# A patch gather on TensorE: from f32 one-hots made on ScalarE to three bf16 parts with one-hots shared between VectorE and ScalarE

## The chip, the core and the metric

The kernel runs on one core of one Trainium2 chip. The metric is the device time of one execution in microseconds (us); less is better. The kernel before took 6811.16 us, the median of three runs (6809.01 to 6819.06).

## What is computed

The input is `x`, 8 images of 32 channels and 128 x 128 pixels. Two layers follow each other. The reference, cut to the part that the change touches and to the outline of the rest:

```python
def _patch_match_stack(x):                 # x is group-normalised
    for dy in range(-2, 3):                # 25 offsets
        for dx in range(-2, 3):
            d = ((x - sh) ** 2).sum(1, keepdims=True)   # sh: x shifted by (dy, dx), clipped
            costs.append(_conv(d, ones, pad=1))         # 3x3 box sum
    _, idx = jax.lax.top_k(-cost, K)       # K = 8 cheapest offsets of each pixel
    g = x[:, yy, xx]                       # gather: 8 pixels of 32 channels for each pixel
    return g as [8, 256, 128, 128]
xb = _patch_match_stack(_gn(x))
dct = _conv(xb, dct_w, groups=32)
h = relu(dw3x3(_conv(xb, w1), w2)); h = relu(dw3x3(_conv(h, w3), w4))
wiener = sigmoid(dw3x3(_conv(h, w5), w6))              # 256-channel 1x1 and depthwise 3x3
x = x + _conv(_conv(wiener * dct, inv_dct_w, groups=32), agg_w)   # layer 0
x = x + conv5x5(_gn(x))                                           # layer 1
```

## The kernel before, in words

**Order of the work.** The order of the instructions on TensorE, VectorE and ScalarE is written out by the program, and each of these engines works its list from front to back. `steps` holds 17 steps for each image: 16 blocks of 8 rows and a last short one. One pass of the outer loop treats four depths of the pipeline, `i` in (3, 2, 1, 0): the three pairs of a pointwise and a depthwise convolution of successive steps, and the end of layer 0. In every `i` the loop also places one `unit` of the gather and calls `tick`, which takes work of the next image (its search for offsets) and of layer 1 from four queues: D (VectorE), A (ScalarE), P and Q (TensorE). Work on D carries a planned cost, and `total` (line 992) sets how much of it a tick releases. In `turn`, used before the main loop and wherever `until` waits for a condition, each queue is run once.

**Search.** For each image `prep` normalises the pixels (`xn`, f32, four strips of 32 rows on the partitions) and pushes `sources`. `squares` makes 36 pairs of differences (L421 on VectorE, squares on ScalarE, sums over channels on TensorE); `costs` makes four blocks of box sums, each with 32 calls of max and max_index (L513, L514). `places` turns the indices into numbers of rows of a gather table and sends them to DRAM as bf16 (`idxd`, L549).

**Gather table.** `sources` transposes the pixels in f32, eight chunks of four rows with four transposes each (L390), copies them from PSUM (`xs`, L392), writes them to DRAM pixel by pixel (`xl`, L394), and from there makes `xtd` with 16 + 2 DMAs (L402, L406). `xtd` holds, for every row, 16 column positions (`QW`) of 11 column tiles (`NT`), each tile 12 columns wide (`TW`). These DMAs are issued on GpSimd's queue, like most of the kernel's. The step that follows in the queue is taken once for each chunk.

**Gather.** A unit is four rows and half (`g`) of the eight offsets. `gather_load` brings the table of the rows (`xt`, 8 rows x 16 positions on 128 partitions, L567) and two broadcasts of the indices to all partitions (`ib`, 128 x 1024 bf16 each, L582). `gather_select` makes the one-hot on ScalarE in two passes, max(0, 1 - (index - partition)^2): a square with the partition number as bias (L596), and a Relu that writes f32 (`sel`, L597). `gather_pixels` multiplies: 11 column tiles x 4 strips of 32 output partitions, each an f32 matmul of a 128 x 32 table with 48 one-hot columns (L611; 32 columns in the last tile), and copies the result to `xb` (L618). An f32 matmul stands in the trace as two records, so a unit has 88. The main loop selects unit u+1, loads unit u+3 and multiplies unit u. There are 64 units for each image, 512 in all.

**What reads it.** `xb` feeds the first pointwise convolution (L649, L673) and, by way of DRAM, the grouped 1x1 convolution at the end (L769, L788). The depthwise convolutions are split: half of the channels on TensorE (L729), half as eight multiply-adds on VectorE (L703).

Of the kernel before, what the change touches and what calls it, by code (L numbers as in the profile page):

```python
# [15 lines left out]
P = 128  # L16
# [4 lines left out]
NS = H // R  # L21
TW = 12
NT = 11
QW = TW + 4
HR = 38
HX = W + 4
SR = 6
EPS = 1e-5


# [12 lines left out]
def bm3d_conv_preact(  # L43
# [88 lines left out]
    nc.vector.memset(neg, 0.0)  # L132
    nc.vector.tensor_copy(neg[:, 28:32], cst[:, C_B + 24 : C_B + 24 + P : 32])
    nplace = const.tile([P, 1], F32, name="nplace")
    nc.vector.tensor_scalar(nplace, cst[:, C_Q : C_Q + 1], -1.0, None, op0=ALU.mult)

# [245 lines left out]
    def sources(b, xn):  # L382


        xl = dram.tile([H, W, C], F32, name=f"xl_{b}", tag="xl")
        for r in range(0, 32, 4):
            yield "P", 0
            pt = ps_x.tile([P, 4, P], F32, name=f"px_{b}_{r}", tag="x")
            for q in range(4):
                nc.tensor.transpose(pt[:, q], xn[:, 3 + r + q, 2 : 2 + W], ident)  # L390
            xs = work.tile([P, 4, P], F32, name=f"xs_{b}_{r}", tag="ct")
            nc.scalar.copy(xs, pt)  # L392
            for q in range(4):
                nc.gpsimd.dma_start(  # L394
                    xl.rearrange("(g r) x c -> r x g c", g=4)[r + q],
                    xs[:, q].rearrange("p (g c) -> p g c", c=C),
                )
        xt = xtd[b] = dram.tile([H, QW, NT, C], F32, name=f"xtd_{b}", tag="xtd")
        for j in range(QW):
            ta, tz = (1 if j < 2 else 0), (NT if j < 10 else NT - 1)  # L400
            xa = TW * ta + j - 2
            nc.gpsimd.dma_start(  # L402
                xt[:, j, ta:tz], xl[:, xa : xa + TW * (tz - ta - 1) + 1 : TW]
            )
        for ja, jz, t, at in ((0, 2, 0, 0), (10, QW, NT - 1, W - 1)):
            nc.gpsimd.dma_start(  # L406
                xt[:, ja:jz, t], xl[:, at : at + 1].to_broadcast([H, jz - ja, C])
            )

# [109 lines left out]
    def places(b, idx, i):  # L519


        if i == 0:
            idxd[b] = dram.tile([4, 8, K * 4, W], BF16, name=f"idxd_{b}", tag="idxd")
        yield "D", 2.6
# [8 lines left out]
        for lim in (10.0, 15.0, 20.0):  # L533
# [5 lines left out]
            o3,  # L539
            cst[:, C_BASE : C_BASE + 4].unsqueeze(1).to_broadcast([P, 64, 4]),  # L540
            ALU.add,
        )
        yield "P", 0
        for h in range(2):
            pt = ps_x.tile([P, 512], F32, name=f"pi_{b}_{i}_{h}", tag="x")
            nc.tensor.transpose(pt[:, :P], o[:, h * P : (h + 1) * P], ident)
            li = work.tile([P, P], BF16, name=f"li_{b}_{i}_{h}", tag="li")
            nc.scalar.copy(li, pt[:, :P])
            nc.gpsimd.dma_start(  # L549
                idxd[b][2 * h : 2 * h + 2, 2 * i : 2 * i + 2].rearrange("g s k x -> g (s k) x"),  # L550
                li,
            )
        ready.add((b, i))
        if i == 3:
            ready.add(b)

    ready = set()
    xbs, xts, ibs, selss = {}, {}, {}, {}

    def gather_load(b, s4, g):  # L560

        if g == 0:

            xt = xts[b, s4] = work.tile([P, NT, C], F32, name=f"xt_{b}_{s4}", tag="xt", bufs=3)
            ys = [min(max(4 * s4 - 2 + r, 0), H - 1) for r in range(8)]
            if ys[7] - ys[0] == 7:
                nc.gpsimd.dma_start(  # L567
                    xt.rearrange("p t c -> p (t c)"),
                    xtd[b][ys[0] : ys[0] + 8].rearrange("r x t c -> (r x) (t c)"),
                )  # L570
            else:
                for r, y in enumerate(ys):
                    nc.gpsimd.dma_start(
                        xt[QW * r : QW * (r + 1)].rearrange("p t c -> p (t c)"),
                        xtd[b][y].rearrange("x t c -> x (t c)"),
                    )
        for k2 in range(2):
            ib = work.tile(
                [P, 2, 4, W], BF16, name=f"ib_{b}_{s4}_{g}_{k2}", tag="ib", bufs=5
            )  # L580
            k0 = 4 * g + 2 * k2
            nc.gpsimd.dma_start(  # L582
                ib.rearrange("p k y x -> p (k y x)"),
                idxd[b][s4 // 8, s4 % 8, 4 * k0 : 4 * k0 + 8]
                .rearrange("k x -> (k x)")
                .partition_broadcast(P),
            )
            ibs[b, s4, g, k2] = ib

    def gather_select(b, s4, g, k2=(0, 1)):  # L590
        for k2 in k2:
            sel = work.tile(
                [P, 2, 4, W], F32, name=f"sel_{b}_{s4}_{g}_{k2}", tag="sel", bufs=4
            )
            ib = ibs.pop((b, s4, g, k2))
            nc.scalar.activation(ib, ib, AF.Square, bias=nplace)  # L596
            nc.scalar.activation(sel, ib, AF.Relu, scale=-1.0, bias=1.0)  # L597
            selss[b, s4, g, k2] = sel

    def gather_pixels(b, s4, g):  # L600

        n, h = s4 // 2, s4 % 2
        if h == 0 and g == 0:
            xbs[b, n] = xbp.tile([P, 2, R, W], F32, name=f"xb_{b}_{n}", tag="xb")
        xb, xt = xbs[b, n], xts[b, s4]
        sels = [selss.pop((b, s4, g, k2)) for k2 in range(2)]
        pg = ps_x.tile([P, 4, W], F32, name=f"pg_{b}_{s4}_{g}", tag="x")
        for t in range(NT):
            xa, xz = TW * t, min(TW * (t + 1), W)
            for j in range(4):  # L610
                nc.tensor.matmul(  # L611
                    pg[C * j : C * (j + 1), :, xa:xz],
                    xt[:, t],
                    sels[j // 2][:, j % 2, :, xa:xz],
                    start=True,
                    stop=True,
                )
        nc.scalar.copy(xb[:, g, 4 * h : 4 * h + 4], pg)  # L618
        if h == 1 and g == 1:
            nc.gpsimd.dma_start(xbd[b][:, :, R * n : R * (n + 1)], xb)  # L620
# [305 lines left out]
    def middle(b, mr):  # L926
# [40 lines left out]
    units = [  # L967
        (b, 2 * n + h, g) if n < NS else None
        for b, n in steps
        for h in range(2)  # L970
        for g in range(2)
    ]
# [3 lines left out]
    def unit(stage, u, *rest):  # L976
        if 0 <= u < len(units) and units[u]:
            if stage is gather_load:
                at = (units[u][0], units[u][1] % 8 // 2)
                until(lambda: at in ready, 4.0)  # L980
            stage(*units[u], *rest)
# [9 lines left out]

    total = 5.5 + 3.3 + 36 * 1.95 + 4 * 4.6 + 32 * 1.85 + 4 * 2.6 + 4 * 3.6 + 6.6
    owed = [0.0]
# [19 lines left out]
    with tc.manual_schedule(engines=ORDERED):  # L1013
# [19 lines left out]
        for s in range(len(steps) + 2):  # L1033
# [10 lines left out]
            for i in (3, 2, 1, 0):  # L1044
# [22 lines left out]
                if s < len(steps):  # L1067
                    unit(gather_select, u + 1, (0,))
                    unit(gather_load, u + 3)
# [11 lines left out]
                if s < len(steps):  # L1081
                    unit(gather_select, u + 1, (1,))
                    u += 1
# [72 lines left out]
```

## Time and profile before

| | |
|---|---|
| median of the runs | 6811.16 us |
| the profiled execution: span from its first to its last instruction | 6807.3 us |
| what lies between that span and the median | 3.9 us |
| TensorE matmul busy | 6354.3 us, 93% |
| VectorE busy | 5860.4 us, 86% |
| ScalarE busy | 5064.6 us, 74% |
| GpSimd busy (it issues most of the DMAs) | 3246.7 us, 48% |
| mean granted TensorE clock | 0.973 |
| DMA | 1021.41 MB, 150 GB/s |

The profile gives one execution. A busy share is the time in which an engine had an instruction in flight; a row of the profile gives a line of the kernel, the engine, the operation, output<-input, how often, then busy time and the mean duration of one. A matmul's mean duration is its flight, not the distance between two. After the bar stands the idle time of the engine in front of these instructions and what ended it. The chain is followed back from the last instruction to whatever released each one; its shares tell where a saved microsecond would have counted in this execution. The windows give the busy time of each engine in a stretch of 50 us.

### The profile page before, as it was taken

How to read it: one execution, taken by the hardware profiler on the slowest of the kernel's cores; microseconds unless marked ns; L12 is line 12 of the kernel's file. 1: busy time of each engine (PE TensorE's matmuls, PEld its weight loads, DVE VectorE, ACT ScalarE, POOL GpSimd, SP SyncE). 2: the span in 40 equal slices, each digit the busy share in tenths (PEclk: the TensorE clock that was granted, in tenths of full speed). 3: DMA queues.
4: the chain of work that ended last, by engine and by line, in shares of the span. 5: the costliest groups of instructions: out<-in, count | busy, mean ns of one | idle time of the engine just before them, and what ended most of it. 6: DMA issues, size and time to landing. Idle time of an engine off the chain costs nothing.

```text
span 6807.3 us, 257036 instructions
## 1 busy us (share of the span) xinstructions
PE 6354.3 (93%) x113378; PEld 3352.8 (49%) x113378; DVE 5860.4 (86%) x8822; ACT 5064.6 (74%) x6698; POOL 3246.7 (48%) x5351
## 2 busy tenths in 40 slices
PE   5798899999999999999999999999999999999997
PEld 1454454554545455454554455545555454455553
DVE  7789988989889898898988888899888899877776
ACT  5787778777687777877777777877769777687772
POOL 7354446444464444544445444454436554344334
PEclk8899999999999999999999999999999999999998
DMA  4566656666566675666756656566665666566653
GB/s 90 143 153 153 151 149 154 159 152 158 147 156 155 144 169 135 163 151 152 167 135 158 161 146 169 138 165 159 149 150 151 162 156 152 138 170 157 154 151 80
DMA packets 809627, 1021.41 MB, mean 150 GB/s; under 512 B 255456, under 2 KB 619936, under 8 KB 808512
## 3 DMA queue, kind: packets, MB, share of 16 engines
q0 software_dynamic: 422432, 745.61, 42.9%
q1 hardware_dynamic: 383568, 258.11, 17.4%
q8 instruction: 892, 14.61, 0.9%
q10 hardware_dynamic: 2512, 1.25, 0.1%
q14 instruction: 223, 1.83, 0.1%
HBM read 553.25 MB, written 217.01 MB: 113 GB/s over the span
## 4 chain that ended last, share of the span: by engine, by line
PE 55%; DVE 23%; ACT 8%; DMA 6%; issue 5%; POOL 3%; SPq 0%; ACTq 0%; DVEq 0%; POOLq 0%
PE pw L729 18%; DVE acc L703 15%; PE pv L649 13%; PE p L673 12%; PE pg L611 4%; DVE df L421 3%; PE pc L788 2%; DMA t<-t 2%; PE p L902 2%; ACT df L429 2%; ACT ib L596 2%; DVE idx L514 1%; PE pa L809 1%; DMA xf<-xbd 1%; DVE acc L796 1%
## 5 line engine op out<-in xcount | busy, mean ns | idle before, releaser
L703 DVE SCALAR_TENSOR_TENSOR acc<-tv,dwv,acc 128x1024 f32<-128x1024 f32 (+3 forms) x3264 | 4032.9, 1237 | 249.6 <-ACT acc L700 140.3
L729 PE MATMUL pw<-t,dwd 96*32 96x254 f32 (+7 forms) x31680 | 2144.1, 422 | 84.7 <-issue 40.5
L729 PEld LDWEIGHTS pw<-t,dwd 96*32 96x32 f32 (+1 forms) x31680 | 1103.9, 111 | 906.6 <-issue 440.7
L582 POOL DMA_DIRECT2D ib<-idxd x1024 | 570.7, 558 | 1796.5 <-ACT sel L597 1620.6
L596 ACT ACTIVATE ib<-ib,nplace 128x1024 bf16<-128x1024 bf16 x1024 | 1170.1, 1143 | 9.5 <-DMA ib<-idxd 9.5
L597 ACT ACTIVATE sel<-ib 128x1024 f32<-128x1024 bf16 x1024 | 1084.8, 1059 | 32.5
L673 PE MATMUL p<-acc,lw 128*32 128x256 f32 x16768 | 989.1, 381 | 25.3 <-ACT tv L657 22.7
L649 PE MATMUL pv<-acc,lw 128*128 128x512 f32 (+1 forms) x2112 | 980.7, 607 | 29.9 <-DVE acc L796 27.4
L769 POOL DMA_DIRECT2D xf<-xbd x1088 | 650.2, 630 | 304.2 <-PE pc L788 87.0
L673 PEld LDWEIGHTS p<-acc,lw 128*32 128x32 f32 x16768 | 556.2, 111 | 454.9 <-ACT tv L657 62.5
L657 ACT COPY tv<-pv 128x512 f32<-128x512 f32 (+2 forms) x784 | 438.1, 578 | 390.4 <-PE pv L649 374.2
L611 PEld LDWEIGHTS pg<-sel,xt 128*32 128x32 f32 x45056 | 575.5, 111 | 252.1 <-issue 54.2
L429 ACT ACTIVATE df<-df 128x786 f32<-128x786 f32 (+2 forms) x576 | 468.0, 859 | 291.9 <-DVE df L421 289.2
L611 PE MATMUL pg<-sel,xt 128*32 128x48 f32 x45056 | 592.7, 207 | 80.4 <-ACT sel L597 46.0
L421 DVE TENSOR_TENSOR df<-xn 128x786 f32<-128x786 f32 (+2 forms) x576 | 532.5, 976 | 116.0 <-PE pd L436 109.2
L742 ACT ACTIVATE acc<-pw 128x512 f32<-128x512 f32 (+2 forms) x808 | 439.9, 573 | 249.7 <-PE pw L729 249.0
L649 PEld LDWEIGHTS pv<-acc,lw 128*128 128x128 f32 x2112 | 384.2, 193 | 475.6 <-issue 398.1
L707 ACT ACTIVATE acc<-acc 128x1024 f32<-128x1024 f32 (+3 forms) x408 | 416.8, 1022 | 229.7 <-DVE acc L703 229.5
L680 ACT COPY t<-p 128x512 f32<-128x512 f32 x800 | 424.6, 570 | 127.7 <-PE p L673 125.7
L700 ACT ACTIVATE acc<-tv,dwv 128x1024 f32<-128x1024 f32 (+3 forms) x408 | 454.5, 1114 | 52.6 <-PE pa L809 35.0
L649 PE MATMUL pv<-xb,lw 128*128 128x512 f32 x1024 | 477.4, 609 | 0.0
L673 PE MATMUL p<-xb,lw 128*32 128x256 f32 x8192 | 468.1, 380 | 4.4 <-DVE xy L914 4.4
(151 smaller groups left out, 5782.5 us busy)
## 6 DMA issues: line engine op xcount, KB each, us to landing
ib<-idxd POOLq DMA_DIRECT2D x1024, 256.0 KB, 4.4
xbd<-xb POOLq DMA_DIRECT2D x128, 1024.0 KB, 6.7
xf<-xbd POOLq DMA_DIRECT2D x960, 128.0 KB, 7.3
t<-t SPq DMA_DIRECT2D x792, 128.0 KB
t<-t SPq DMA_DIRECT2D x384, 256.0 KB
tv<-tv SPq DMA_DIRECT2D x384, 130.0 KB
xt<-xtd POOLq DMA_DIRECT2D x240, 176.0 KB, 4.6
xl<-xs POOLq DMA_DIRECT2D x256, 64.0 KB, 2.6
```

The lines of the kernel that those rows point to most:

```text
L421: nc.vector.tensor_sub(df[:, :, ca:cz], xn[:, r0 : r0 + SR, ca:cz], xn[:, r0 + dy : r0 + dy + SR, ca + dx : cz + dx],)
L429: nc.scalar.activation(df[:, :, ca:cz], df[:, :, ca:cz], AF.Square)
L582: nc.gpsimd.dma_start(ib.rearrange("p k y x -> p (k y x)"), idxd[b][s4 // 8, s4 % 8, 4 * k0 : 4 * k0 + 8] .rearrange("k x -> (k x)") .part ...
L596: nc.scalar.activation(ib, ib, AF.Square, bias=nplace)
L597: nc.scalar.activation(sel, ib, AF.Relu, scale=-1.0, bias=1.0)
L611: nc.tensor.matmul(pg[C * j : C * (j + 1), :, xa:xz], xt[:, t], sels[j // 2][:, j % 2, :, xa:xz], start=True, stop=True,)
L649: nc.tensor.matmul(ps[:, :hr], lhsT[:, g, P:CK], src(g)[:, h : h + hr], start=g == 0, stop=g == 1,)
L673: nc.tensor.matmul(ps[C * r : C * (r + 1), e, :nb], lhsT[:, g, s], rows[:, r : r + 4 * nb - 3 : 4], start=g == 0, stop=g == 1,)
L700: nc.scalar.activation(acc, rows, AF.Copy, scale=tap)
L703: nc.vector.scalar_tensor_tensor(acc, rows, tap, acc, op0=ALU.mult, op1=ALU.add)
L729: nc.tensor.matmul(pt[u][C * j : C * (j + 1), ka:kz, :nb, xa:xz], dwd[0:hi, i - 1, u, j, dx + 1], t[0:hi, j, ka:kz, :nb, xa + dx : xz + dx ...
L769: nc.gpsimd.dma_start(xf[p : p + C, m, j0:j1], src[g, m, (h + m + 1) % 2, :, :, ya:yz])
```

## The change

The table is kept as three bf16 parts of each f32 number: the number rounded to bf16, the rest rounded to bf16, and the rest of that. Eight bits of mantissa each, they add up to the f32 number, and a one-hot picks each exactly; the three matmuls of a pixel add up in PSUM. `sources` makes the parts with two casts on ScalarE and two subtractions on VectorE for each chunk, transposes twelve times in bf16, copies twice from PSUM and writes 96 instead of 32 numbers for each pixel. It now goes through six steps of the queues for each chunk (A, D, A, D, P, P) where it went through one. `xtd` has 15 positions of 12 tiles, each 11 columns wide, six for the left half of the columns and six for the right (`HW` = 64); a table fills 120 partitions. It is made with 30 + 2 DMAs.

A unit is now four rows and one half of the columns (`f`), all eight offsets. It has one broadcast `ib` of 128 x 2048 bf16, held in four buffers. The one-hot of the left half is one comparison on VectorE, in place; that of the right half two passes on ScalarE, in place, bf16. A unit's matmuls are 6 tiles x 3 parts x 4 strips = 72, of 88 columns (72 in the last tile). `gather_load` waits, while the program is written out, until `sources` of its image has been placed. The indices are written in twice as many DMAs.

```diff
-TW = 12
-NT = 11
+TW = 11
+NT = 12
+HW = W // 2
+NP = 3
...
     def sources(b, xn):
-        xl = dram.tile([H, W, C], F32, name=f"xl_{b}", tag="xl")
+        xl = dram.tile([H, W, NP * C], BF16, name=f"xl_{b}", tag="xl")
         for r in range(0, 32, 4):
-            yield "P", 0
-            pt = ps_x.tile([P, 4, P], F32, name=f"px_{b}_{r}", tag="x")
-            for q in range(4):
-                nc.tensor.transpose(pt[:, q], xn[:, 3 + r + q, 2 : 2 + W], ident)
-            xs = work.tile([P, 4, P], F32, name=f"xs_{b}_{r}", tag="ct")
-            nc.scalar.copy(xs, pt)
...
+            nc.scalar.copy(parts[0], rows)
+            yield "D", 0.7
+            nc.vector.tensor_sub(rest, rows, parts[0])
+            yield "A", 0
+            nc.scalar.copy(parts[1], rest)
+            yield "D", 0.7
+            nc.vector.tensor_sub(parts[2], rest, parts[1])
+            for q0 in (0, 2):
+                yield "P", 0
+                pt = ps_x.tile([P, 2, 4, NP, C], BF16, name=f"px_{b}_{r}_{q0}", tag="x")
+                for q in range(2):
+                    for s in range(NP):
+                        nc.tensor.transpose(pt[:, q, :, s], parts[s][:, q0 + q], ident_b)
+                xs = work.tile([P, 2, 4, NP * C], BF16, name=f"xs_{b}_{r}_{q0}", tag="xs")
+                nc.scalar.copy(xs, pt.rearrange("p q g s c -> p q g (s c)"))
...
+        sourced.add(b)
...
+        ib = work.tile([P, K, 4, HW], BF16, name=f"ib_{b}_{s4}_{f}", tag="sel", bufs=4)
+        nc.gpsimd.dma_start(
+            ib.rearrange("p k y x -> p (k y x)"),
+            idxd[b][s4 % 8 // 2, s4 // 8 * 2 + s4 % 2, f].rearrange("k x -> (k x)").partition_broadcast(P),
+        )
...
-            nc.scalar.activation(ib, ib, AF.Square, bias=nplace)
-            nc.scalar.activation(sel, ib, AF.Relu, scale=-1.0, bias=1.0)
...
+        if f == 0:
+            if part != 1:
+                nc.vector.tensor_scalar(ib, ib, place, None, op0=ALU.is_equal)
+            return
+        if part != 1:
+            nc.scalar.activation(ib, ib, AF.Square, bias=nplace)
+        if part != 0:
+            nc.scalar.activation(ib, ib, AF.Relu, scale=-1.0, bias=1.0)
...
-        for t in range(NT):
-            xa, xz = TW * t, min(TW * (t + 1), W)
-            for j in range(4):
-                nc.tensor.matmul(
-                    pg[C * j : C * (j + 1), :, xa:xz],
-                    xt[:, t],
-                    sels[j // 2][:, j % 2, :, xa:xz],
-                    start=True,
-                    stop=True,
-                )
+        for t in range(NT // 2):
+            xa, xz = TW * t, min(TW * (t + 1), HW)
+            for s in range(NP):
+                for j in range(4):
+                    nc.tensor.matmul(
+                        pg[C * j : C * (j + 1), :, :, xa:xz],
+                        xt[: 8 * QW, f * (NT // 2) + t, C * s : C * (s + 1)],
+                        sel[: 8 * QW, j : j + 5 : 4, :, xa:xz],
+                        start=s == 0,
+                        stop=s == NP - 1,
+                        skip_group_check=True,
+                    )
...
-                until(lambda: at in ready, 4.0)
+                until(lambda: at in ready and at[0] in sourced, 4.0)
...
-    total = 5.5 + 3.3 + 36 * 1.95 + 4 * 4.6 + 32 * 1.85 + 4 * 2.6 + 4 * 3.6 + 6.6
+    total = 5.5 + 3.3 + 8 * 1.4 + 36 * 1.95 + 4 * 4.6 + 32 * 1.85 + 4 * 2.6 + 4 * 3.6 + 6.6
...
-                    unit(gather_select, u + 1, (0,))
+                    unit(gather_select, u + 1, 0)
...
-                    unit(gather_select, u + 1, (1,))
+                    unit(gather_select, u + 1, 1)
```

## The prediction, as it was made before the result was known

> **What bounds the kernel now.** I read the page's busy times and slices first, then the chain, then rows by shape, then windows.
>
> ```profile
> PE 6354.3 (93%) x113378; PEld 3352.8 (49%) x113378; DVE 5860.4 (86%) x8822; ACT 5064.6 (74%) x6698; POOL 3246.7 (48%) x5351
> PE   5798899999999999999999999999999999999997
> DVE  7789988989889898898988888899888899877776
> ...
> PE 55%; DVE 23%; ACT 8%; DMA 6%; issue 5%; POOL 3%; SPq 0%; ACTq 0%; DVEq 0%; POOLq 0%
> ```
>
> TensorE is busy nearly throughout, except in the first two slices (340 us) and the last. VectorE follows closely. The chain, where a saved microsecond counted, is TensorE for 55% and VectorE for 23%.
>
> ```profile
> 2550.00:2600.00 50.00, 50.00 (x867) 25.93 (x869) 40.10 (x35) 31.18 (x42) 18.36 (x35) 1.00 0.53 142
> 2700.00:2750.00 50.00, 45.64 (x807) 24.46 (x806) 42.40 (x46) 49.51 (x70) 29.68 (x48) 1.00 0.46 112
> 2850.00:2900.00 50.00, 46.85 (x872) 24.48 (x868) 48.26 (x88) 36.26 (x47) 21.24 (x32) 1.00 0.57 137
> ```
>
> Windows of 50 us; columns: PE, PEld, DVE, ACT, POOL. One is full on TensorE, one on ScalarE (49.51), one nearly on VectorE (48.26). So three engines take turns; the change relieves two and loads the third.
>
> ```profile
> L611 PE MATMUL pg<-sel,xt 128*32 128x48 f32 x40960 | 559.6, 208 | 70.8 <-ACT sel L597 46.0 <-issue 18.6 <-DVE acc L796 3.0
> ...
> L596 ACT ACTIVATE ib<-ib,nplace 128x1024 bf16<-128x1024 bf16 x1024 | 1170.1, 1143 | 9.5 <-DMA ib<-idxd 9.5
> L597 ACT ACTIVATE sel<-ib 128x1024 f32<-128x1024 bf16 x1024 | 1084.8, 1059 | 32.5
> ...
> L367 DVE TENSOR_SCALAR xn<-xn,mr_a 128x5016 f32<-128x5016 f32 x8 | 23.6, 2952 | 0.4
> ...
> L582 POOL DMA_DIRECT2D ib<-idxd x1024 | 570.7, 558 | 1796.5 <-ACT sel L597 1620.6 <-ACT acc L742 53.0 <-DMA xf<-xbd 26.2
> ```
>
> Matmuls of 208 ns overlap: what counts is the distance of their starts. ScalarE spends 2255 us on one-hots. GpSimd's 1620.6 us behind them are mostly slack, as the ib transfer keeps ScalarE waiting for only 9.5.
>
> **The change, part by part.** I price each part by its busy time times the share that such work has on the chain, as it is spread over the span. That sum is a floor, since paths beside the chain do not shorten; part 7 is for that.
>
> 1. *Matmuls of the gather.* In one unit at 3027 us the records' starts come in fours, one for each strip: 42.5 ns for a four of 48 columns, 28 ns for 32. That is 0.88 ns for each column, and the unit takes 10 x 2 x 42.5 + 2 x 28 = 906 ns. Afterwards it has 18 fours, 15 of 88 columns and 3 of 72: 1536 columns. No bf16 matmul is in this trace. Lower end: the shortest four seen, 18 x 28 = 504 ns. Upper end: f32's price for each column, 1359 ns. I take half of it, 680 ns, because bf16 has half the bytes. Saved 226 ns x 512 = 116 us. The chain holds 268 us of the gather's 464 (58%): **-67** (-119 to +135).
>
> The Trainium skill speaks against any such stream of small matmuls (TensorE: Matmul & The Clock Gate, "Wait — 56ns, not 53.3ns?"): starts are never under some 25 ns apart. By it a unit of 72 would take 1.8 us and one of 88 would take 2.2 us; the trace has 0.906 us with records 6 to 18 ns apart, so the measurement decides.
>
> 2. *One-hots on ScalarE.* 1024 pairs of 1143 + 1059 ns go. 256 pairs of twice the length come. ScalarE's rows for L707 (1024 elements 1060 ns, 384 elements 526 ns) give 0.83 ns an element, so 1.14 + 0.85 and 1.06 + 0.85 us: 1001 us. Removed: 1254 us, 56%. The chain's pieces add up to 117 us of L596 and 32 of L597: **-83** (-149 if all goes, 0 if another wait stands there).
>
> 3. *One-hots on VectorE.* 256 comparisons of 2048 bf16. VectorE's TENSOR_SCALAR rows (5016 f32 2952 ns, 256 f32 302 ns) give 0.56 ns an element and 0.16 us for each call. At f32's price a comparison is 1.30 us. The upper end is the multiply-add's price, 1.04 ns an element (1024 in 1284 ns, 128 in 351): 2.35 us. The lower end is the 0.16 us alone. I take half of f32's, again by bytes: 0.73 us, 187 us in all, 23% of it on the chain: **+43** (+9 to +138). Behind it in VectorE's order stand the tick's work and the eight multiply-adds. It waits for a broadcast loaded two units (some 25 us) earlier, with 4.4 us to landing, so not for that.
>
> The skill (VectorE: DVE Perf Modes, "The perf-mode tier table") has 693 ns for this size, which would make part 3 +41. The skill also speaks against it (SBUF — State Buffer, "SBUF: two separate sides"): such a two-port operation keeps GpSimd from writing descriptors. At 693 ns that would be up to 177 us of GpSimd held, +5 at GpSimd's 3% of the chain. No row of this trace shows it.
>
> 4. *Making the parts.* 128 subtractions of 512 elements on VectorE at 0.69 us (from L485: 1040 in 1238 ns, 910 in 1102 ns) are 88 us: +20. On ScalarE each chunk has two casts of 0.63 us and two copies of 768 elements of 0.80 us for one of 0.57: 64 x 2.3 = 147 us, at 8%: +12. The transposes change little: a chunk's four f32 ones take 0.66 us, twelve of 128 bf16 columns at 0.44 ns 0.68. Sum **+32** (0 to +90).
>
> 5. *DMA and GpSimd.* 512 broadcasts fewer at 558 ns are -286 us; the table takes 30 issues of some 0.83 us and two more instead of 17.5 us, +72 over eight images; twice the index writes, 64 at 0.8, +52. A freed buffer is now awaited from the matmuls of unit u-1, which come before the pass awaited now. The chain has 23 us of issuing and 42 us of landing of ib. I take **-20**. The ends are -65, and +40 if ib and xf queue behind the table's longer issue block (its 16 issues stood on the chain once, 15.6 us).
>
> 6. *The head.* `sources` takes four turns a chunk now, so image 0's table is ready only after 32 turns, and nothing is gathered before. By the order of the instructions the first multiply-add comes after 128 instead of 96 pairs of max and max_index (0.42 us each), one more `places` (2.8), 16 subtractions and 4 comparisons: 30 us more VectorE. GpSimd's 26.5 us of table issues, hidden at 82 to 99 us before, now end on the path: issues, landing (4.4), eight xt loads (3.9) and their landing (3.5) are 38 us after the last chunk.
>
> ```profile
> 177.83 1.97 PE L502 MATMUL pt<-cst,dsum 128*128 128x128 f32 x8
> 199.95 0.66 PE L546 MATMUL pi<-cst,oc 128*128 128x128 f32 x2 [20.16 <-DVE oc L537]
> 200.54 1.94 PE L611 MATMUL pg<-sel,xt 128*32 128x48 f32 x88
> 202.41 4.73 PE L649 MATMUL pv<-xb,lw 128*128 128x512 f32 x8
> ```
>
> The main loop starts at 202 us here, after a wait for `places`. I expect some 240. About 10 us come back, as the search's last block no longer holds up the first steps: **+30** (+15 to +60).
>
> 7. *Less room on VectorE.* It gets 275 us more, 2.1 us in each 50; TensorE loses 0.9. Of 19 windows from 2500 to 3450 us, five (as the third above) would then have VectorE over 50 or longest by 1 to 5 us. They lose some 12 us against the others, 85 over the main loop, of which parts 3 and 4 hold 63: **+30** rounded up for waits back and forth (0 to +100).
>
> Sum: -67 - 83 + 43 + 32 - 20 + 30 + 30 = -35. The profiled span is 6807.3 us, and 3.9 us lie between it and the median; these stay. Forecast 6811.2 - 35 = **6776 us**.
>
> **Rivals.**
> - *VectorE becomes the bound (slower).* One mechanism: the comparison costs f32's price or more, beside engines in lockstep. For it: windows with 48 of 50 us busy. Against: bf16 has half the bytes. With part 7 growing alike, about 0.35 of each added microsecond counts; 35 / (256 x 0.35) = 0.39, so it decides from 1.12 us a comparison. At 1.30 us it gives 6827; at 2.35 VectorE has 6550 us to do, at 93% use 7040.
> - *bf16 columns cost what f32's records do (slower).* Part 1 becomes +135: 6978 us. Against: f32 is two records for each matmul, so its price is no floor.
> - *No change.* What TensorE gains, the other engine of each stretch keeps, or the head takes more: 6811.
> - *ScalarE was the hidden releaser (faster).* Its in-order passes delay the copies that TensorE and VectorE wait for. For it: the second window, and 140.3 us of VectorE's waits on L700. Its load falls by 22% net; if all of its 546 us on the chain fall alike (-120 where parts 2 and 4 have -71) and part 7 is nothing, 6811 - 35 - 49 - 30 = 6697.
> - That the comparison is not on VectorE can be excluded: the order has one for each left unit there and two passes for each right one on ScalarE.
>
> **How the numbers follow.** Forecast (6740 to 6800) 0.40, ScalarE rival 0.16, no change 0.12, VectorE rival 0.23, bf16 rival 0.06, a head beyond +60 or a clash of DMAs (up to 6880) 0.03. From 6650 to 6900 leaves out about 0.2: the far ends of parts 1 and 3 and of the ScalarE rival. 0.2% (14 us) is about what a measurement can tell. Faster by more: 0.56 (the forecast and the ScalarE rival); within: 0.12; slower: 0.32.
>
> **What would show it.** Part 1: a unit's matmuls within 0.7 us, 0.9 to 1.4 if wrong. Part 2: ScalarE busy near 3960 us. Part 3: comparisons of 0.7 us; VectorE busy near 6135 us, with its share of the chain up and TensorE's down. Part 6: the first L649 (now L689) near 240 us. The forecast is wrong if comparisons take over 1.1 us, if TensorE's idle time in the main loop grows by more than its matmuls lose, or if GpSimd's table issues stand on the chain for every image.

## The result, and the profile after

The changed kernel takes 6850.36 us (median of seven runs) against 6811.16 us. The ratio is 1.0067, with a 95% interval of 1.0047 to 1.0088: 0.7% slower, where the forecast had 0.5% faster. The profiled execution took 6846.71 us, its span is 6844.9 us. Below, "us of 6811" is (ratio - 1) x 6811; the change is +46 by it (+32 to +60).

The page of the changed kernel, the lines that answer to those shown of the kernel before:

```profile
PE 6330.6 (92%) x105698; PEld 3300.5 (48%) x105698; DVE 6107.3 (89%) x9211; ACT 4064.6 (59%) x5354; POOL 3103.0 (45%) x5015
...
PE   4699999999999999999999999999999999999997
...
DVE  8699979999899998999989999899989999887886
...
PE 46%; DVE 29%; DMA 9%; ACT 4%; issue 4%; POOL 4%; SPq 0%; DVEq 0%; POOLq 0%; ACTq 0%
```

ScalarE has lost 1000 us and GpSimd 144, VectorE has gained 247; the parts had forecast 1107, 162 and 275. On ScalarE the changed rows came out as priced, but an engine's busy time counts instructions that overlap once: its rows add up to 5386 us before and 4306 after, its busy times are 5065 and 4065, so 80 us of overlap went with the removed passes. TensorE's busy time fell by 24 us only. On the chain TensorE and ScalarE hold less, VectorE and DMA more.

The rows of the changed lines, groups by shape (after the bar: busy us, mean ns of one):

```profile
L634 ACT ACTIVATE ib<-ib,nplace 128x2048 bf16<-128x2048 bf16 x256 | 511.0, 1996 | 10.6 <-DMA ib<-idxd 10.6
L636 ACT ACTIVATE ib<-ib 128x2048 bf16<-128x2048 bf16 x256 | 488.7, 1909 | 0.1
L650 PE MATMUL pg<-ib,xt 120*32 120x88 bf16 x30720 | 484.0, 214 | 68.1 <-DMA xt<-xtd 31.7 <-ACT ib L636 18.6 <-ACT bc L883 6.3
L440 POOL DMA_DIRECT2D xtd<-xl x240 | 200.1, 844 | 4.6 <-DMA xl<-xs 4.2 <-DMA xtd<-xl 0.3
L631 DVE TENSOR_SCALAR ib<-ib,cst 128x2048 bf16<-128x2048 bf16 x256 | 193.9, 758 | 33.8 <-DMA ib<-idxd 33.8
L426 ACT COPY xs<-px 128x768 bf16<-128x768 bf16 x128 | 100.7, 788 | 4.9 <-PE px L424 3.8 <-issue 1.1
L414 DVE TENSOR_TENSOR rest<-xn,part 128x512 f32<-128x512 f32 x64 | 43.7, 683 | 0.0
```

Every duration that was forecast for these rows, the matmuls aside, came out within 4%: passes 1.996 and 1.909 us (1.99 and 1.91), comparisons 0.758 (0.73), copies 0.788 (0.80), subtractions 0.683 (0.69).

Where did the time go? First the start of the main loop, TensorE's instructions in order of time (start, duration, idle time before them):

```profile
223.93 3.07 PE L650 MATMUL pg<-ib,xt 120*32 120x88 bf16 x148 [31.71 <-DMA xt<-xtd]
...
242.17 2.08 PE L689 MATMUL pv<-xb,lw 128*128 128x512 f32 x2
```

The first `pv` stands at 242.17 us instead of 202.41. From there to the end of the span it is 6602.7 us, against 6604.9 before. So the loss is as long as the growth of the head, and the main loop, which by the forecast should have gained 75 us (the 65 of parts 1 to 5 and 7 and the 10 that part 6 expected back), gained two: TensorE's busy time in it fell by 25 us, and its idle time grew by 23. One image in the middle of each kernel, before first, then after (columns: length, then busy us of PE, PEld, DVE, ACT, POOL):

```profile
1847.20:2675.70 828.50, 791.65 (x14173) 419.68 (x14171) 730.35 (x1100) 632.00 (x837) 403.35 (x666) 0.98 0.63 154
```

```profile
2722.40:3552.70 830.30, 786.95 (x13214) 414.88 (x13211) 760.88 (x1145) 506.23 (x669) 385.09 (x624) 0.98 0.65 160
```

ScalarE does 126 us less in an image, VectorE 31 more, TensorE 5 less, and the image takes as long. What follows asks what ate the gain.

### The profile page after: what moved, and what is told of

The parts are those of the page before. It is cut to its first block, busy times and chain, and to the rows that moved or that the text cites. A ratio compares the mean times of both kernels' runs of the same rounds, so it can differ in the third digit from the quotient of the medians.

```text
span 6844.9 us, 240175 instructions
## 1 busy us (share of the span) xinstructions
PE 6330.6 (92%) x105698; PEld 3300.5 (48%) x105698; DVE 6107.3 (89%) x9211; ACT 4064.6 (59%) x5354; POOL 3103.0 (45%) x5015
## 4 chain that ended last, share of the span: by engine, by line
PE 46%; DVE 29%; DMA 9%; ACT 4%; issue 4%; POOL 4%; SPq 0%; DVEq 0%; POOLq 0%; ACTq 0%
DVE acc L743 19%; PE pw L769 15%; PE pv L689 11%; PE p L713 10%; DMA t<-t 3%; PE pg L650 3%; PE pc L828 2%; DVE df L461 2%; DMA xf<-xbd 2%; POOL xtd L440 2%; PE pd L476 1%; DVE idx L554 1%; DVE acc L836 1%; PE pa L849 1%; PE p L942 1%
## 5 line engine op out<-in xcount | busy, mean ns | idle before, releaser
L769 PEld LDWEIGHTS pw<-t,dwd 96*32 96x32 f32 (+1 forms) x31680 | 1083.7, 111 | 934.8 <-issue 479.3
L713 PEld LDWEIGHTS p<-acc,lw 128*32 128x32 f32 x16768 | 574.2, 111 | 416.6 <-issue 51.3
L621 POOL DMA_DIRECT2D ib<-idxd x512 | 291.1, 569 | 854.7 <-PE pg L650 642.1
L650 PEld LDWEIGHTS <-xt 120*32 120x32 bf16 x36864 | 509.7, 99 | 249.6 <-issue 140.2
L720 ACT COPY t<-p 128x512 f32<-128x512 f32 x800 | 440.2, 574 | 312.1 <-PE p L713 300.0
L650 PE MATMUL pg<-ib,xt 120*32 120x88 bf16 (+1 forms) x36864 | 545.7, 213 | 73.4 <-DMA xt<-xtd 31.7
L658 ACT COPY xb<-pg 128x512 f32<-128x512 f32 x512 | 301.2, 588 | 450.7 <-PE pg L650 449.2
L634 ACT ACTIVATE ib<-ib,nplace 128x2048 bf16<-128x2048 bf16 x256 | 511.0, 1996 | 10.6 <-DMA ib<-idxd 10.6
L636 ACT ACTIVATE ib<-ib 128x2048 bf16<-128x2048 bf16 x256 | 488.7, 1909 | 0.1
```

Of the source, the lines that this page charges most:

```text
L636: nc.scalar.activation(ib, ib, AF.Relu, scale=-1.0, bias=1.0)
L650: nc.tensor.matmul(pg[C * j : C * (j + 1), :, :, xa:xz], xt[: 8 * QW, f * (NT // 2) + t, C * s : C * (s + 1)], sel[: 8 * QW, j : j + 5 : 4 ...
L713: nc.tensor.matmul(ps[C * r : C * (r + 1), e, :nb], lhsT[:, g, s], rows[:, r : r + 4 * nb - 3 : 4], start=g == 0, stop=g == 1,)
L769: nc.tensor.matmul(pt[u][C * j : C * (j + 1), ka:kz, :nb, xa:xz], dwd[0:hi, i - 1, u, j, dx + 1], t[0:hi, j, ka:kz, :nb, xa + dx : xz + dx ...
```

## The experiments

Eighteen kernels ran. Each was compared with the kernel before on its own chip. They change the kernel after (e, a), the kernel before (b), or the faster form that the experiments led to (e7, e8, f).

### Prices at the changed kernel's order

The first four tested whether the head is the loss, and what each side of the loop is worth.

**e1_head.** Image 0's table is made in fewer steps of the queues: all of a chunk in one.

```diff
-            yield "A", 0
+            yield ("A" if b else "P"), 0
...
-            yield "D", 0.7
+            if b:
+                yield "D", 0.7
...
```

> Of the changed kernel, only the head is altered: image 0's sources goes through one queue step for each chunk, as before the change, the other images as in the changed kernel. Theory HEAD (the 39 us lost are all in the head: 242 us to the first pointwise matmul instead of 202, while the rest takes 6603 us in both): the first L689-type matmul near 205 to 215 us and a time of 6815 to 6825 us. Theory ELASTIC (work taken out of the head is paid again in image 0's loop, as the search then overlaps it): the head shortens but the time stays at 6840 to 6850 us.

Measured: 6865.03 us, ratio 1.0068 (1.0046 to 1.0090), the first `pv` at 238.4. The edit did not do what it was for: cast, subtraction, cast, subtraction in one step wait for each other on two engines that work in order, a chunk takes about 10 us, and the start moved by 4 us only. It does not decide between the theories. Still, its table is issued by 152 us instead of 214, the first gather matmul stands at 188.6 instead of 223.9, and then TensorE waits for the search of the first image:

```profile
236.25 0.66 PE L590 MATMUL pi<-cst,oc 128*128 128x128 f32 x2 [15.98 <-DVE oc L581]
```

In the kernel before this `pi` stands at 199.95. So an early table alone does not bring the head back when its making holds up the search.

**e2_all_act and e3_no_left.** The left one-hots go to ScalarE too (two passes), or are left out altogether, so that the left half is not gathered.

```diff
         if f == 0:
-            if part != 1:
-                nc.vector.tensor_scalar(ib, ib, place, None, op0=ALU.is_equal)
             return                  # e3; in e2 the return goes too
```

> Of the changed kernel, the one-hot of the left columns is made on ScalarE too, by the same two passes; VectorE loses its 256 comparisons (194 us), ScalarE gets 1000 us back (5065 us, as before the change). Theory VECTOR (in the loop the gains on TensorE and ScalarE are eaten by VectorE's 281 us more): about 0.3 of 194 us comes back, 6785 to 6805 us, less up to 40 us for ScalarE's return. Theory DMA (the table's longer block on GpSimd's queue and the later xf transfers eat them): 6845 to 6890 us, no gain or a loss by ScalarE's load.

> Of the changed kernel, the one-hot of the left columns is left out: the matmuls of the left half take the indices as they come, so this half of the gather is not computed. It takes 194 us from VectorE and gives nothing to another engine. Theory VECTOR: 6785 to 6800 us. Theory DMA: 6840 to 6850 us, as VectorE's work isn't what holds the loop.

Measured: e2 6844.91, ratio 1.0057 (1.0030 to 1.0083); e3 6812.04, ratio 0.9996 (0.9980 to 1.0011). The comparisons cost 48 us of 6811 (1.0067 less 0.9996) where 43 were forecast. The two passes in their place, 1000 us of ScalarE by their rows, cost 42 (e2 less e3): at this order moving the left one-hots from ScalarE to VectorE bought nothing.

**e5_one_part.** Only the first of the three parts is multiplied; the other two matmuls are left out.

```diff
-            for s in range(NP):
+            for s in range(1):
...
-                        stop=s == NP - 1,
+                        stop=True,
```

> Of the changed kernel, only the first of the three bf16 parts is multiplied, so a unit has 24 matmuls instead of 72 (two parts of each gathered number are left out). TensorE loses about 0.53 us in each of 512 units, 270 us. Theory VECTOR: VectorE at 89% holds the loop, TensorE's work counts for little, 6800 to 6830 us. Theory TENSOR (TensorE is still the bound, and the gain of 0.10 us a unit instead of the forecast 0.23 is what is missing): 0.46 to 0.6 of 270 us, 6690 to 6730 us.

Measured: 6814.94, ratio 1.0002 (0.9986 to 1.0018). Twelve of 18 fours go, 12 x 44 ns x 512 = 270 us of TensorE by its starts, and 44 us come back: 16%, not 58%. In its page and its waits:

```profile
PE 6145.5 (90%) x81122; PEld 2964.3 (43%) x81122; DVE 6103.6 (89%) x9211; ACT 4038.2 (59%) x5354; POOL 3102.9 (45%) x5015
```

```profile
PE pw L769 <- DMA t<-t: 122.8, 40, 8.7
PE pi L586 <- DVE oc L577: 99.1, 18, 10.2
PE pc L828 <- DVE acc L836: 95.5, 19, 7.1
```

The columns of a wait are us in total, how many, and the longest. TensorE now waits for DMA and VectorE: 122.8, 99.1 and 95.5 us, against 34.8, 66.9 and 53.5 in the changed kernel; some 20 us of the growth may be this execution's own, as the profiled one took 6837.27 against a median of 6814.94. Its granted clock is lower too, 0.949 against 0.969.

**e6_both.** Both are left out, e3's comparisons and e5's two parts.

```diff
         if f == 0:
-            if part != 1:
-                nc.vector.tensor_scalar(...)
             return
...
-            for s in range(NP):
+            for s in range(1):
```

> The changed kernel without the comparisons of the left one-hots and with the first of the three parts multiplied alone; both are left out of the computation. Alone the first gave -38 us and the second -36. Theory SUM (each engine has stretches of its own): 6850 - 74, near 6776 us. Theory TURNS (the engines stand close to each other, what one is relieved of the next holds): together they give clearly more than the sum, 6690 to 6750 us.

Measured: 6722.69, ratio 0.9862 (0.9838 to 0.9887). That is 140 us of 6811 under the changed kernel, where 48 and 44 alone make 93 (unrounded). So without the comparisons the fours are worth 91 us, and without the fours the comparisons 95. VectorE and TensorE each keep much of what the other is spared.

### Turns without work

**b1_steps, b3_total, b4_turns.** The kernel before, with parts of the change's order and none of its work: b4 has the change's six steps of the queues for each chunk, five of them empty, and the wait for the table, b3 the raised `total`, b1 both.

```diff
         for r in range(0, 32, 4):
+            yield "A", 0              # b1, b4
+            yield "D", 0.7
+            yield "A", 0
+            yield "D", 0.7
+            yield "P", 0
             yield "P", 0
...
-    total = 5.5 + 3.3 + 36 * 1.95
+    total = 5.5 + 3.3 + 8 * 1.4 + 36 * 1.95      # b1, b3
```

> The kernel before with nothing of the change but its order in the queue: each chunk of `sources` takes four more empty turns, the comparison's place of the main loop waits for image 0's table as in the changed kernel, and no work is added or taken away. Theory STEPS (the 39 us of the head come from the 32 turns before the table of image 0 is ready): the first pv near 230 to 240 us instead of 202, the rest of the run as before, so 6840 to 6850 us. Rival WORK (the head grows because of the added work itself: subtractions, casts, the 30 table issues): the first pv within 202 to 212 us and 6811 to 6822 us.

> The kernel before with only `total` raised by 11.2, as the change does (4.8% more queue work released by a tick); no turns and no gate added. The run with turns, gate and total together gave 6919 us, +102, of which 30 at the head and about 15 in each later image. Theory PACE (the faster release does it, since it bunches the search in the early blocks of an image): 6870 to 6900 us, the head at 202. Rival TURNS (the 32 more turns of `sources` do it): 6805 to 6825 us.

> The kernel before with the 32 more empty turns of `sources` and the gate, but with `total` as it was. Theory TURNS: the first pv near 232 us and about 15 us more in each later image, 6880 to 6925 us. Theory PACE: the head alone, 6840 to 6850 us.

Measured: b1 6918.80, ratio 1.0147 (1.0125 to 1.0169); b3 6835.01, ratio 1.0037 (1.0022 to 1.0051); b4 6819.90, ratio 1.0014 (1.0001 to 1.0026). The head's theory is shown by b4: with empty steps alone the main loop starts late.

```profile
232.74 4.46 PE L655 MATMUL pv<-xb,lw 128*128 128x512 f32 x8
```

That is 30 of the 40 us that the changed kernel's head grew by. But b4's loop is 28 us shorter than the one before, and b1's 90 us longer, with the same work (in the profiled executions, 9 us under b4's median and 11 over b1's). Both theories of the loop fell: neither PACE nor TURNS alone makes b1's +100, the two together do. One of its waits shows the sort of thing that happens, b1 first, then the kernel before:

```profile
DVE acc L709 <- ACT acc L706: 295.4, 159, 36.3
```

```profile
DVE acc L703 <- ACT acc L700: 140.3, 131, 5.6
```

VectorE's multiply-adds wait for ScalarE's pass twice as long in all, and once for 36.3 us, where 5.6 was the longest. Why this pair of edits is bad and each alone is not stays open. What it means for the rest: **kernels whose queues are filled in another order cannot be compared to better than some 1%**, even at equal work.

**a1_total.** The changed kernel with `total` as before.

```diff
-    total = 5.5 + 3.3 + 8 * 1.4 + 36 * 1.95
+    total = 5.5 + 3.3 + 36 * 1.95
```

> The changed kernel with `total` as it was before, nothing else. Theory PACE: the loop gives back some 10 to 15 us for each image, 6740 to 6780 us. Theory TURNS: 6835 to 6860 us, as the changed kernel.

Measured: 6865.04, ratio 1.0075 (1.0050 to 1.0099), the same as the changed kernel. The raised `total` is not the loss.

**a2_pipe.** All of the change's work, `sources` in ten rounds of two steps, 20 steps instead of 48.

```diff
+        for c in range(10):
+            yield "A", 0
+            # casts of chunk c (first part) and c - 1 (second part)
+            yield "P", 0
+            # transposes, copies, writes of c - 2; subtractions of c - 1 and c
...
-    total = 5.5 + 3.3 + 8 * 1.4 + 36 * 1.95
+    total = 5.5 + 3.3 + 36 * 1.95
```

> The changed kernel with all of its work, but with `sources` in two turns of the queue for each chunk and no more: in one turn the casts of chunk k and k-1, in the next the transposes of k-2 and the subtractions of k-1 and k, 20 turns instead of 48; `total` as it was. Theory TURNS (order, not work, ate the change's gain): the first pv near 215 to 222 us and 12 to 18 us less in each later image, 6720 to 6750 us. Theory WORK (comparisons and parts ate it): the head's 20 to 25 us alone come back, 6820 to 6830 us.

Measured: 6817.57, ratio 1.0003 (0.9992 to 1.0015). The main loop starts at 211.14 us and takes 6609.8: the head's 31 us come back, the loop gains nothing. This is what theory WORK expected: it is not the order alone that eats the gain.

### Making and moving the parts

**e7_one_part_all.** One bf16 part everywhere. This kernel rounds the pixels to bf16: the second and third parts, their subtractions, casts, transposes, bytes and matmuls are left out.

```diff
-NP = 3
+NP = 1
...
+            yield "A", 0
+            nc.scalar.copy(part, rows)
+            yield "P", 0
+            # four transposes, one copy, four writes
```

> The changed kernel with one bf16 part instead of three everywhere: pixels are rounded to bf16, the second and third parts are left out with their subtractions, casts, transposes, half of the table's issues and 12 of 18 fours of a unit. The turns of `sources` are two a chunk again, the comparison on VectorE stays. Theory STEPS: the first pv back near 205 us, -36 for it, -36 for TensorE's fours as in the run with one part, -10 to -25 for subtractions (88 us of VectorE), issues and transposes: 6755 to 6770 us. If the head doesn't come back: 6790 to 6800.

Measured: 6614.56, ratio 0.9710 (0.9683 to 0.9737). It is 2.9% faster than the kernel before, at less precision of the gathered pixels, and it beat every number I had for it by 140 us and more. The issues of the table were as many as in the changed kernel, not half as the expectation has it, so they were no part of it. The next three runs split it.

**f1_thrice.** e7 with each matmul issued three times, each starting its sum anew: TensorE's 18 fours are back.

```diff
-            for s in range(NP):
+            for s in range(3):
...
-                        start=s == 0,
-                        stop=s == NP - 1,
+                        start=True,
+                        stop=True,
```

> The kernel with one bf16 part everywhere (6615 us), each of its matmuls issued three times, so that TensorE has the changed kernel's 18 fours in a unit again; all else as in it. Theory TENSOR (TensorE's fours are what the one-part kernel won by): +100 to +150, 6715 to 6765 us. Theory PARTS (making and moving the parts were the price): +35 to +60, 6650 to 6675 us.

Measured: 6720.13, ratio 0.9856 (0.9838 to 0.9874). The fours cost 99 us of 6811 here, the low end of theory TENSOR. This kernel has the change's matmuls, its comparisons, its passes and its 30 table issues, but does not make and move three parts. It is 98 us faster than the kernel before.

**f2_bytes.** e7 with its part written three times side by side: the copies, the writes, the table and its loads have the changed kernel's size.

```diff
-            xs = work.tile([P, 4, 4, C], BF16)
-            nc.scalar.copy(xs, pt)
+            xs = work.tile([P, 4, 4, 3 * C], BF16)
+            nc.scalar.copy(xs, pt)      # each pixel's 32 numbers three times
```

> The kernel with one bf16 part everywhere (6615 us), the part written three times side by side into the table, so that the copies out of PSUM, the writes, the table and its loads have the changed kernel's size (1066 instead of 975 MB); one part is multiplied, and there are no subtractions and no second and third casts. Theory BYTES: +60 to +120, 6675 to 6735 us. Rival: the bytes are hidden, +0 to +20, and the subtractions, casts and their order are what is left: 6615 to 6635 us.

Measured: 6713.81, ratio 0.9842 (0.9822 to 0.9863): +90 us of 6811 for 1062 instead of 975 MB and copies of three times the size (1436 instead of 581 ns; ScalarE +61 us). TensorE's waits, e7 first, then f2 (its profiled execution took 6736.92, 23 above its median):

```profile
PE pw L757 <- DMA t<-t: 92.5, 41, 12.0
```

```profile
PE pw L760 <- DMA t<-t: 139.9, 48, 9.2
...
PE pc L819 <- DVE acc L827: 98.9, 20, 15.0
```

And the landing of the transfers, in the same order (KB each, us to landing):

```profile
ib<-idxd POOLq DMA_DIRECT2D x512, 512.0 KB, 5.5
...
xt<-xtd POOLq DMA_DIRECT2D x240, 90.0 KB, 5.1
```

```profile
ib<-idxd POOLq DMA_DIRECT2D x512, 512.0 KB, 6.0
...
xt<-xtd POOLq DMA_DIRECT2D x240, 270.0 KB, 6.2
```

Larger table loads land later, the broadcasts beside them as well, and the shifted copies `t<-t`, which have nothing to do with the gather, keep TensorE waiting for 47 us more. The `pc` wait, on VectorE, was 22.1 us in e7. Bytes and copies were not taken apart, so how much of the 90 is each stays open.

**a3_pipe_one.** a2 with the first part multiplied alone, as in e5 (the same diff).

> The pipelined form of the changed kernel (6818 us) with the first of three parts multiplied alone; the parts are made and moved as before, the other two matmuls are left out. Theory VECTOR (VectorE's load keeps most of what TensorE saves): -30 to -50, 6770 to 6790 us. Theory TENSOR (its saving counts more in another order): -90 or more, under 6730 us.

Measured: 6767.74, ratio 0.9934 (0.9915 to 0.9952). The fours give 47 us here. Against f2, which has the same bytes and the same matmuls, it is 63 us of 6811 slower: the subtractions, a second cast, and 12 instead of 4 transposes for each chunk, with the order that they need. Some 13 of them are a later start (the first `pv` at 211.83 instead of 198.88).

**e8_one_act.** e7 with the left one-hots on ScalarE (e2's diff).

> The kernel with one bf16 part everywhere (6615 us) with the left one-hots on ScalarE too (two passes), as in the first column of runs where all one-hots of the changed kernel went there: VectorE loses 194 us, ScalarE gains 1000. VECTOR (VectorE, busy for 91%, holds this kernel): 6540 to 6580 us. Rival (ScalarE's passes cost as much as they free): 6600 to 6630 us.

Measured: 6640.71, ratio 0.9741 (0.9724 to 0.9759), no faster than e7: in the faster kernel, too, the comparisons on VectorE cost no more than the 890 us of ScalarE that they save.

### Prices at the order of the kernel before

**b2_fewer.** 3 of 11 column tiles are multiplied, the rest of the gather is left out.

```diff
-        for t in range(NT):
+        for t in range(3):
...
-        nc.scalar.copy(xb[:, g, 4 * h : 4 * h + 4], pg)
+        nc.scalar.copy(
+            xb[:, g, 4 * h : 4 * h + 4].rearrange("p y (a x) -> p y a x", x=32),
+            pg[:, :, 0:32].unsqueeze(2).to_broadcast([P, 4, 4, 32]),
+        )
```

> The kernel before with 3 of its 11 column tiles multiplied; the other 8 tiles of the gather are left out, and the copy out of PSUM repeats the first 32 columns, so every other engine has what it had. TensorE loses 18 of 22 fours of a unit, about 8 x 2 x 42.5 = 680 ns x 512 = 350 us. Theory SHARE (a microsecond of the gather on TensorE is worth its 58% on the chain, as the forecast had it): 6811 - 200, near 6610 us. Theory TURNS (another engine of the same stretch takes over, as in the run with one part, where 270 us of TensorE gave 36): 13%, so 6811 - 46, near 6765 us, with TensorE's idle time in the main loop up by about 300 us and VectorE's waits named in it.

Measured: 6682.20, ratio 0.9805 (0.9780 to 0.9830). 7 tiles of 2 x 42.5 ns and one of 2 x 28, by 512, are 333 us of TensorE; 133 came back, 40%, between the two theories.

**b6_one_pass.** The square of the one-hots is left out, the second pass runs on the raw indices.

```diff
-            nc.scalar.activation(ib, ib, AF.Square, bias=nplace)
```

> The kernel before without the first of the two passes of the one-hots on ScalarE (the square is left out, the second pass runs on the raw indices), so 1170 us of ScalarE less and nothing else changed. Theory CHAIN (the chain's 117 us of this line come back): near 6700 us. Theory ELASTIC (as at the changed kernel's order, 3.3%): near 6775 us. If ScalarE is no limit at all: 6811 us.

Measured: 6664.11, ratio 0.9776 (0.9750 to 0.9802): -153 us of 6811 for 1170 us of ScalarE, more than the 117 that this line held on the chain and than either theory expected. Some 10 of them are an earlier start (the first `pv` at 192.65).

```profile
PE 6309.9 (95%) x113378; PEld 3344.9 (50%) x113378; DVE 5857.9 (88%) x8822; ACT 3984.9 (60%) x5674; POOL 3246.6 (49%) x5351
...
PE 69%; DVE 20%; DMA 5%; issue 3%; ACT 2%; POOL 2%; SPq 0%; DVEq 0%; POOLq 0%; ACTq 0%
```

TensorE is at 95% and has 69% of the chain: what ScalarE gave up went to TensorE. VectorE's wait for TensorE's sums (`df` behind `pd`) falls from 109.2 us to 49.0, its wait for ScalarE (`acc`) from 140.3 to 103.6.

**b5_bytes.** A table of 16 instead of 32 numbers a pixel; half of the channels is left out, TensorE multiplies as much.

```diff
-        xl = dram.tile([H, W, C], F32)
+        xl = dram.tile([H, W, 16], F32)     # likewise xtd and xt
```

> The kernel before with a gather table of 16 instead of 32 numbers for each pixel: half of the channels is left out of the writes of the pixels, of the table and of its loads, and the matmuls read the next 16 numbers instead, so that every engine has what it had; about 42 of 1021 MB go. Theory BYTES (1.1 us for a MB, as between the runs with one part): -45, 6760 to 6780 us. Rival (the transfers are hidden in this kernel, and the price in the one-part kernel was that of its copies or its order): 6805 to 6820 us.

Measured: 6820.37, ratio 1.0008 (0.9994 to 1.0022). 43 MB less give nothing. In the kernel before these bytes are hidden; in e7, where ScalarE and TensorE do less, 88 MB more and their copies cost 90 us. So one price for a byte does not fit both kernels.

## Why the prediction was wrong

**Where the gain went.** Three differences split the change's +46 us of 6811:

| from | to | what it adds | us of 6811 | forecast |
|---|---|---|---|---|
| before | f1 | bf16 matmuls, one-hots, table issues (parts 1, 2, 3, 5, 7) | -98 | -67 - 83 + 43 - 20 + 30 = -97 |
| f1 | a2 | making and moving three parts (part 4) | +100 | +32 |
| a2 | after | 48 instead of 20 steps of the queues, `total` (part 6) | +44 | +30 |

The first `pv` of f1, then of a2, beside 202.41 us before and 242.17 after:

```profile
194.11 4.74 PE L677 MATMUL pv<-xb,lw 128*128 128x512 f32 x8
```

```profile
211.14 5.21 PE L695 MATMUL pv<-xb,lw 128*128 128x512 f32 x8
```

From there to the end of the span it is 6604.9 us before, 6526.8 in f1, 6609.8 in a2 and 6602.7 after. So 17 of the 100 are a later start, which the prediction books under part 6, and some 83 are in the main loop; of the 44, 31 are the start.

**The step that failed is part 4, "Making the parts": +32 (0 to +90); it measured about +100, some 83 of it in the main loop.** I priced its subtractions and casts by VectorE's and ScalarE's shares, and said that the transposes change little. Half as many bytes again for the pixels, the table and its loads (1021 to 1066 MB) had no term at all: part 5 counted issues and not bytes. With one part multiplied, bytes and copies cost 90 us (f2 less e7), making the other parts 63 (a3 less f2); with all fours on TensorE the two cost 100 together, perhaps because they then fall partly beside its work. Orders differ between f1 and a2 (16 and 20 steps), and order alone moved the kernel before by up to 1.5%, so the 100 is not sharp. Against order as the whole of it stand two things: f2 and e7 have one order, and a2 and the changed kernel, with 20 and 48 steps, have loops that differ by 7 us. f1 also moves 43 MB less than the kernel before; by b5 that was worth nothing there.

The other steps, one by one:

1. *Matmuls.* The mechanism held, its size and its share did not. A four of 88 columns takes 42 to 45 ns, about 0.5 ns a column, not 0.44; a unit's first to last start fell from 899 to 798 ns, from first start to the next line's from 1024 to 893. Saved: 0.10 to 0.13 us of 0.226. And a microsecond of it was worth 16% (e5) to 40% (b2), not 58%: 512 x 0.13 x 0.16 to 0.40 is 11 to 27 us for the 67. The share on the chain said where TensorE was the last, not how far behind it the others were.
2. *ScalarE.* Undervalued. 153 us for 1170 (b6) are 0.13 for each, so 1254 would be 164 for the 83. The rival of the hidden releaser, with its -120, came closer for this engine: in b6 waits on other engines fell too. At the changed kernel's order the same passes were worth 0.04 (e2 less e3), so this price too is spent once.
3. *Comparisons.* Right: 0.758 us for 0.73, 48 us for 43, though 95 where TensorE holds less. The Trainium skill (VectorE: DVE Perf Modes, "The perf-mode tier table") has 693 ns for a bf16 operation of this kind and size; here it is 758, and that decides. Its warning that such operations keep GpSimd from its descriptors (SBUF — State Buffer, "SBUF: two separate sides") shows in the trace, at a small size. The means hide it: an issue of the broadcast takes 569 ns, of `xf` 623, against 558 and 630 before. But 216 of GpSimd's issues overlap a comparison by more than 50 ns; the 89 of `xf` among them take 759 ns and the other 999 take 611, the 14 of the table 1056 against 825. An estimate from these rows is some 40 us of GpSimd in all; what it cost in time no run shows.
4. See above.
5. *GpSimd.* Its rows came out as priced: 291.1 us for the broadcasts, 200.1 for the table. No run has them alone. One sign of being wrong that the prediction named came in part: the table's issues stand on the chain for five images (119 us, 2% of it), where the kernel before had them there for one. But f1 has them there too, with 3%, and is 98 us faster than the kernel before, so they are not what the gain went to.
6. *The head.* Right: 242 for "some 240", and b4 shows that empty steps make 30 of the 40. But "about 10 us come back" is neither shown nor excluded; in b4 28 did, by its profiled execution.
7. *Less room on VectorE.* The interaction is real and larger than a rounding: 140 - 93 = 47 us between the comparisons and the fours (e6). In the first line of the table it is within the sum.

Parts 1 and 2 were wrong in opposite directions, and 8 of the 98 are an earlier start that no part forecast; so the first line of the table is right to a microsecond by luck.

The rivals: that VectorE becomes the bound from 1.12 us a comparison did not decide, as they take 0.758. That bf16 columns cost what f32's do is out. "No change" describes the main loop, +46 the whole. The range held the time; the sign was missed.

## What to carry to other kernels

A share of the chain is not a price: for TensorE's fours it said 58%, and 16 to 40% came back; ScalarE's first pass held 117 us of it, and leaving the pass out gave 153. Where three engines take turns, a relief is worth what the next engine leaves, and two reliefs together can be worth half as much again as apart (140 against 93 us). When one number is kept as three, count the making, the bytes and the steps of the queues besides the matmuls; here they took 100 and 44 us of a gain of 98. Before engine work is blamed, run the old kernel with the new order and no work: empty steps, with the planned release that belongs to them, moved this one by up to 1.5%.

## What the runs showed of the hardware

- The granted clock of TensorE goes with how busy TensorE is: 0.981 at 95% (b6), 0.973 at 93% (before), 0.965 at 92% (e7), 0.949 at 90% (e5). In the traces it is 1.0 or 0.5 at any one time; at 0.5 the `pv` matmuls of 512 columns start 853 ns apart, at 1.0 429. It is 0.5 for 428 us of the changed kernel's span and for 704 of e5's, and e5's busy time on TensorE is only 185 us less, where the starts that it leaves out make 270. So part of a saving on TensorE is given back; what that is worth in time was not measured by itself.
- With a larger gather table, transfers that have nothing to do with it land later: `ib` after 6.0 instead of 5.5 us (f2 against e7), with 158 instead of 147 GB/s on the core; TensorE's waits for `t<-t` grow by 47 us, though the longer copies may have a part in that. In the kernel before, 43 MB less gave nothing.
- DMA issues on GpSimd that overlap one of VectorE's bf16 comparisons take longer: `xf` 759 against 611 ns (changed kernel), 810 against 619 (f1).
